# Regrouping the value and score products of layer 2 into four 32-wide groups, and moving its output product, in a four-layer cross-attention kernel

## The chip, the cores and the metric

The kernel runs on one core of a Trainium2 chip. The metric is the time of one execution on the device in microseconds (us), as the median of three runs. All arithmetic is in fp32. In this profile one fp32 matrix product appears as two MATMUL records and two weight loads; counts below are counts of records unless "product" is written.

## The reference

Input: `x` (4 sequences of 1024 rows, 256 wide), one context of 77 rows per sequence, and for layer 2 a weight and a mask for each score. Four layers follow one another; each has 16 heads.

- Layer 0: causal self-attention with the context appended, then a feed-forward block.
- Layer 1: a linear attention over the context beside a windowed self-attention (heads of 16).
- Layer 2, cut to what matters:

```python
q = (x @ Wq.T + bq)           # 16 heads of 16 columns
k = (ctx @ Wk.T + bk);  v = (ctx @ Wv.T + bv)      # 77 rows
scores = einsum('bhqd,bhkd->bhqk', q, k) / sqrt(16)
scores = where(mask, -inf, scores * attention_weights)
out = einsum('bhqk,bhkd->bhqd', softmax(scores), v)
x = layernorm(x + out @ Wo.T + bo) * gamma + beta
```

- Layer 3: rms norm, cross-attention with the same context with heads of 64, output product, and the sum with its input.

## The kernel before

The kernel first does layer 0 (to about 1090 us) and layer 1 (to about 1713 us), in steps of one sequence and four heads. Small jobs for later layers are spread over these steps by a planner: `jobs0(b, quad)` lists the jobs of layer 0's step for sequence `b` and heads group `quad`, each a generator with the number of its pieces and the part of the step in which they are due. Two of these jobs prepare layer 2 in DRAM, both in step (0, 0): `values2` multiplies the contexts with `Wv` and writes the values to `kept_v`, and `keys2` writes the keys to `kept_k`, four times, each time masked (`hsel4`) to every fourth head.

Layers 2 and 3 run together, in slots (`slot23`). Slot `i` works on row tile `i` of 128 rows in layer 2 (32 tiles) and on tile `j = i - 12` in layer 3. Each engine executes its instructions in the order in which the slot writes them; no scheduler changes it. A layer-2 tile passes through six slots:

- Slot `i`, `score2`: q times keys on TensorE into two PSUM tiles of two banks each (`pair_tile`, two buffers), multiplied with the weights by VectorE (L1545) into `s`, a buffer of 128 x 1232 (16 heads of 77), and masked (L1550). Then `maxima2` (L1554, L1558).
- Slot `i + 1`: `exps2` on ScalarE, 16 instructions (L1563); `sums_of` on VectorE (L1567, L1570); `divided` on GpSimd (L1574).
- Slot `i + 3`: `turned_into(p3, "pT2")`: ten transposes on TensorE (psT, L1375) in three groups, each evicted by ScalarE into `pT` (L1376).
- Slot `i + 4`: `values_of2`: values times `pT`, into `pvT`, copied to `oT` by ScalarE (L1593).
- Slot `i + 5`: `out2`: `oT` times `Wo` into `po2`; `add2` adds it to `x` on VectorE (L1602), then GpSimd adds `bo` (L1603).

Layer 3 in the same slots: `score3` (TensorE 16 records from G, then VectorE L1626 and L1627 for each of two halves), `exp3` on ScalarE (L1643), `sums_of` and `divided` one slot later, then `turned_into(c2, "pT3")` (the same lines L1375, L1376) and `out3` (20 records from U and pT, added to `x` at L1639) two slots later. `po2` and `po3` share one PSUM buffer. `psT`, `pvT` and other small PSUM tiles share a pool of three buffers (`sm`). From slot 9 on, `between` (called through `more()`, once in four slots for four tiles) does the layer norm of layer 2 and the rms norm of layer 3: bn_stats on VectorE, powers on GpSimd (L293), ScalarE (L1502), `xn` on VectorE (L316), transposes, and L1442. `prep2` computes q of the next sequence.

TensorE's order in a slot that has all of this is: transposes of layer 3, `score2`, `out3`, `values_of2`, `score3`, transposes of layer 2, `out2`.

The values lie for `values_of2` as 11 blocks of up to 128 rows of `s` by 128 columns: each row of `s` (one head and one context row) has its head's 16 columns filled and zeros elsewhere. `score2` makes four products per tile, each with 64 rows of q (four heads) against keys that are masked to one head in each of four blocks, 308 columns.

Of the kernel before, what the change touches and what calls it, by code (L numbers as in the profile page):

```python
# [17 lines left out]
P = 128  # L18
# [13 lines left out]
def tile_xattn_seq(ctx: ExitStack, tc: tile.TileContext, d: dict, out: bass.AP):  # L32
# [13 lines left out]
    def mm(o, lhsT, rhs, start=True, stop=True, **kw):  # L46
        n = 1
        for k in rhs.shape[1:]:
            n *= k
        put[0] += n / 600.0  # L50
        nc.tensor.matmul(o, lhsT, rhs, start=start, stop=stop, **kw)  # L51
# [475 lines left out]
    def pair_tile():  # L527
        return big.tile([P, 2, 512], F32, name="ps", tag="big")
# [403 lines left out]
    kept_g = dram.tile([P, 2, 8, 2, NS], F32, name="kept_g")  # L932
    kept_u = dram.tile([NB, H, S, D], F32, name="kept_u")

    HALF, DIAG = HH * S * P, S * P + DH
    kept_v = dram.tile([NB, 2, HH * DIAG], F32, name="kept_v")
    stg = wpool.tile([P, 1024], F32, name="stg", tag="s7")
    turn = [0]

# [25 lines left out]

    def values2():

        n = NB * 2 * HH * DIAG // P // 8
        nc.gpsimd.memset(stg[:, 0:n], 0.0)
        nc.sync.dma_start(  # L970
            out=kept_v.rearrange("b e x -> (b e x)").rearrange("(p k n) -> p k n", p=P, n=n),
            in_=stg[:, 0:n].unsqueeze(1).to_broadcast([P, 8, n]),
        )
        yield
        for b in range(NB):
            pk = sm.tile([S, D], F32, name="pk", tag="sm")
            for c in range(2):
                mm(pk, ctxT[:, b, c, :], l2["Wv"][:, c, :], start=(c == 0), stop=(c == 1))
            v = place(3, NS)[:S, 0:D]
            nc.vector.tensor_tensor(v, pk, rows["bv2"][:S], ALU.add)  # L980
            for e in range(2):
                to = kept_v[b, e].rearrange("(j x) -> j x", x=DIAG)[:, 0 : S * P]
                nc.sync.dma_start(
                    out=to.rearrange("j (s p) -> s j p", p=P)[:, :, 0:DH],
                    in_=v[:, P * e : P * e + P].rearrange("s (j r) -> s j r", r=DH),
                )
            yield

    def keys2():
# [376 lines left out]
    def rows_in(c):  # L1366
        return P if c < NC - 1 else HSIZE
# [10 lines left out]
    def new_scores(tag, bufs):  # L1378
        s = late.tile([P, P * NC], F32, name=tag, tag=tag, bufs=bufs)
        nc.gpsimd.memset(s[:, HK:], 0.0)  # L1380
        return s
# [27 lines left out]

    def loads2(b):  # L1410

        V = late.tile([P, NC + 1, P], F32, name="V2", tag="V2", bufs=2)
        lo, hi = [kept_v[b, e, 0:HALF].rearrange("(r n) -> r n", n=P) for e in range(2)]

        k = HH * S % P
        nc.gpsimd.memset(V[:, 4:6, :], 0.0)
        nc.sync.dma_start(
            out=V[:, 0:4, :], in_=lo[0 : 4 * P].rearrange("(c p) n -> p c n", p=P)
        )
        nc.sync.dma_start(out=V[0:k, 4, :], in_=lo[4 * P :])  # L1420
        nc.sync.dma_start(out=V[k:P, 5, :], in_=hi[0 : P - k])
        nc.sync.dma_start(
            out=V[:, 6:10, :], in_=hi[P - k : 5 * P - k].rearrange("(c p) n -> p c n", p=P)
        )
        nc.sync.dma_start(out=V[0:HSIZE, 10, :], in_=hi[5 * P - k :])
        shared["v2", b] = V
        yield

    def half_rows(e):
        return slice(64 * e, 64 * e + 64)  # L1430
# [95 lines left out]
    def score2(a, i):  # L1526

        b, t = a["b"], a["t"]
        qT, kb = shared["b2", b], shared["k2"]
        assert shared["ready2"] >= b  # L1530
        fs, mk = shared.pop(("side", i))
        if i + 1 < NB * NT:
            load_sides(i + 1)
        s = a["s"] = new_scores("s2", 4)
        for o in range(2):
            ps = pair_tile()
            for e in range(2):
                r = half_rows(e)
                mm(
                    ps[:, e, 0 : 4 * S].rearrange("p (h s) -> p h s", s=S),  # L1540
                    qT[r, o, P * t : P * t + P],
                    kb[r, o, :, b, :],
                )
            so = slice(o * HH * S, (o + 1) * HH * S)
            nc.vector.tensor_tensor(  # L1545
                s[:, so].rearrange("p (i n) -> p i n", i=2), ps[:, :, 0 : 4 * S],
                fs[:, so].rearrange("p (i n) -> p i n", i=2), ALU.mult,
            )
        sv = s[:, 0:HK]
        nc.vector.copy_predicated(sv, mk, low.to_broadcast([P, HK]))  # L1550
# [33 lines left out]
    def values_of2(a):  # L1584

        V = shared["v2", a["b"]]
        pv = sm.tile([P, 2, P], F32, name="pvT", tag="sm")
        for k in range(NC + 1):
            o, c = (0, k) if k < 5 else (1, k - 1)
            r = slice(0, rows_in(c))  # L1590
            mm(pv[:, o, :], V[r, k, :], a["pT"][r, c, :], start=k in (0, 5), stop=k in (4, NC))
        oT = a["oT"] = late.tile([P, 2, P], F32, name="oT", tag="oT", bufs=2)
        nc.scalar.copy(oT, pv)  # L1593

# [50 lines left out]
    def slot23(i, two, three, more):  # L1645

        n = NB * NT
        j = i - LAG
        if i < n:
            two[i] = dict(zip("bt", divmod(i, NT)))  # L1650
        if 0 <= j < n:
            three[j] = dict(zip("bt", divmod(j, NT)))
        a, p1, p3, p4, p5 = (two.get(i - k) for k in (0, 1, 3, 4, 5))
        c, c1, c2 = (three.get(j - k) for k in range(3))
        if j < 0:
            if p1:
                exps2(p1, range(H))
            score2(a, i)
            more()
            if p5:  # L1660
                out2(p5)
            if p4:
                values_of2(p4)
            maxima2(a)
            more()
            if p3:
                turned_into(p3, "pT2")
            if p5:
                add2(p5)
            more()  # L1670
            if p1:
                sums_of(p1, "den2")
                divided(p1)
            more()
        elif i < n + 5:
            if c2:
                turned_into(c2, "pT3")
            if p1:
                exps2(p1, range(4))
            if a:  # L1680
                score2(a, i)
            if c1:
                sums_of(c1, "den3")
                divided(c1)
            if p1:
                exps2(p1, range(4, 8))
            more()
            if c2:
                out3(c2)
            if p1:  # L1690
                exps2(p1, range(8, 12))
            if a:
                maxima2(a)
            if p4:
                values_of2(p4)
            more()
            if p1:
                exps2(p1, range(12, H))
            if c:
                score3(c, j)  # L1700
            more()
            if p3:
                turned_into(p3, "pT2")
            if c:
                exp3(c)
            if p1:
                sums_of(p1, "den2")
            if p5:
                out2(p5)
                add2(p5)  # L1710
            more()
            if p1:
                divided(p1)
        else:
            if c1:
                sums_of(c1, "den3")
                divided(c1)
            for o in range(2):
                if c2:
                    turned_into(c2, "pT3", (o,))  # L1720
                if c:
                    score3(c, j, (o,))
                if o == 0:
                    more()
            if c2:
                turned_into(c2, "pT3", (2,))
            more()
            if c:
                exp3(c)
            if c2:  # L1730
                out3(c2)
            more()
        two.pop(i - 5, None)
        three.pop(j - 2, None)
# [15 lines left out]
    def jobs0(b, quad):  # L1750
# [7 lines left out]
        if b == 0 and quad == 0:  # L1758
            j.append(Job(later_constants(), 3, 0.0, 0.4))
            j.append(Job(keep("c00", None), 1, 0.1, 0.2, us=0.85))  # L1760
            j.append(Job(values0(0, 0), 8, 0.2, 0.8, us=0.43))
            j.append(Job(other_contexts(), 3, 0.0, 0.1))
            j.append(Job(feature_weights(), 3, 0.5, 1.0))
            j.append(Job(values2(), 5, 0.3, 0.9, us=0.85))
            j.append(Job(keys2(), 4, 0.5, 0.9, us=0.5))
        if (b, quad) == (0, 1):
            j.append(Job(heads3("wk"), 8, 0.0, 1.0, us=1.03))
# [138 lines left out]
    def more():  # L1906
        for e in list(live2):
            gen, each = e[:2]
            for _ in range(each):
                got = next(gen, StopIteration)  # L1910
                if got is StopIteration:
                    live2.remove(e)
                if got:
                    break
# [49 lines left out]
```

## Time and profile before

| What | us |
|---|---|
| median of 3 runs | 2309.76 (2304.88 to 2311.91) |
| the profiled execution | 2310.56 |
| its span in the profile | 2308.8 |
| TensorE busy / VectorE busy / ScalarE busy / GpSimd busy | 2158.3 / 1506.8 / 1027.5 / 652.2 |
| mean granted TensorE clock | 0.982 of full speed |
| layer 2's value products (pvT), busy, 704 records | 90.9 (78.5 + 12.4) |
| layer 2's score products (ps from kb and qT), busy, 256 records | 42.9 |
| first score product of layer 2 / last pvT record | starts at 1724.3 / 2207.3 |

Engines: PE is TensorE's matmul, PEld its weight load, DVE VectorE, ACT ScalarE, POOL GpSimd, SP the engine that issues the DMAs. L51 is the helper through which almost all products go, so products are told apart by their tiles: `po<-U,pT` is `out3`, `po<-w2q,oT` is `out2`, `ps<-G,xT` is `score3`, `ps<-kb,qT` is `score2`. A form such as `128*32 128x192` means 128 rows contracted, 32 weight columns, 192 columns streamed. "Idle before" is the time that an engine stood still ahead of an instruction, and the name behind the arrow is what it waited for.

### The profile page before, as it was taken

What the parts mean: (1) busy time and instruction counts of PE and PEld (TensorE: products, weight loads), DVE (VectorE), ACT (ScalarE), POOL (GpSimd) and SP (SyncE); (2) the same over time, 40 slices, a digit from 0 to 9 for tenths busy, and PEclk for the clock granted to TensorE, in tenths of its full rate; (3) what the DMA queues carried; (4) which work ended last, traced back from release to release, by engine and by line L of the source; (5) the groups of instructions that cost most, each with busy time, mean ns of one, the idle gap of its engine ahead of it and who ended that gap; (6) DMA issues with size and microseconds to landing.
All of it is one profiled execution on the core that took longest, in us unless ns stands there. A gap on an engine that the chain in (4) does not pass through costs nothing.

```text
span 2308.8 us, 41140 instructions
## 1 busy us (share of the span) xinstructions
PE 2158.3 (93%) x16842; PEld 1358.9 (59%) x16874; DVE 1506.8 (65%) x2476; ACT 1027.5 (45%) x1716; POOL 652.2 (28%) x959
## 2 busy tenths in 40 slices
PE   4999999999999999999989999999988899999999
PEld 2544444555555455554556665666656678788877
DVE  3756567755566455754375666777748888788654
ACT  1144444434444444344533444544547655555322
POOL 2011113111131112310152233333333444444432
PEclk9899999999999999999989999999999999999999
DMA  7221121100000000101000010111025412313000
GB/s 217 55 57 68 31 65 41 40 6 15 7 15 2 10 11 6 38 1 19 6 15 6 15 26 16 21 20 20 15 74 152 136 51 68 100 49 95 10 10 17
DMA packets 87858, 93.98 MB, mean 41 GB/s; under 512 B 35714, under 2 KB 77558, under 8 KB 87542
## 3 DMA queue, kind: packets, MB, share of 16 engines
q1 hardware_dynamic: 87670, 91.35, 15.2%
q8 instruction: 133, 2.18, 0.4%
q14 instruction: 55, 0.45, 0.1%
HBM read 55.31 MB, written 18.39 MB: 32 GB/s over the span
## 4 chain that ended last, share of the span: by engine, by line
PE 67%; DVE 15%; ACT 4%; issue 2%; POOL 2%; DMA 0%; DVEq 0%; ACTq 0%; POOLq 0%; SPq 0%
PE ps L51 26%; PE po L51 12%; PE pv L51 6%; PE pp L51 5%; PE ph L51 4%; DVE mpart L672 3%; PE pvT L51 2%; DVE ms L1138 2%; PE ppv L51 2%; PE psT L1375 2%; PE pvw L51 1%; DVE mrow L1142 1%; PE pm L590 1%; PE pt L607 1%; ACT pe L738 1%
## 5 line engine op out<-in xcount | busy, mean ns | idle before, releaser
L51 PE MATMUL ps<-qk 32*128 32x192 f32 (+9 forms) x6528 | 581.8, 428 | 57.9 <-DVE mpart L672 25.1
L738 ACT ACTIVATE pe<-ps 128x1024 f32<-128x1024 f32 (+2 forms) x384 | 363.3, 952 | 589.5 <-PE ps L51 579.9
L51 PEld LDWEIGHTS ps<-qk 32*128 32x128 f32 (+1 forms) x6528 | 315.8, 185 | 295.6 <-issue 75.3
L672 DVE TENSOR_REDUCE mpart<-ps 128x2 f32<-128x1024 f32 (+4 forms) x384 | 331.0, 885 | 241.6 <-PE ps L51 240.8
L741 POOL TENSOR_SCALAR_AFFINE_SELECT pe<-pe 128x256 f32<-128x256 f32 (+1 forms) x192 | 95.2, 497 | 665.3 <-ACT pe L738 664.3
L1214 ACT ACTIVATE pew<-ps 128x768 f32<-128x768 f32 x128 | 103.4, 812 | 196.4 <-PE ps L51 196.4
L1574 POOL TENSOR_TENSOR s<-s,den 128x1232 f32<-128x1232 f32 x64 | 144.2, 2254 | 130.2 <-DVE den L1570 125.2
L1219 POOL TENSOR_SCALAR_AFFINE_SELECT pew<-pew 128x512 f32<-128x512 f32 x128 | 81.9, 640 | 337.7 <-ACT pew L1214 337.6
L1138 DVE TENSOR_TENSOR ms<-ps,maskw 128x768 f32<-128x768 f32 x128 | 122.1, 954 | 69.6 <-PE ps L51 68.1
L51 PE MATMUL po<-U,pT 128*128 128x256 f32 (+1 forms) x640 | 147.2, 385 | 10.8 <-DVE x L1602 7.6
L51 PE MATMUL pv<-pe,va 128*32 128x512 f32 (+3 forms) x1536 | 157.1, 496 | 0.0
L51 PE MATMUL ph<-yT,w 128*128 128x256 f32 x512 | 143.1, 401 | 2.4 <-DVE va L401 1.0
L51 PEld LDWEIGHTS po<-U,pT 128*128 128x128 f32 (+1 forms) x640 | 120.3, 192 | 35.0 <-ACT pT L1376 19.6
L51 PEld LDWEIGHTS po<-w,hT 128*128 128x128 f32 x800 | 111.8, 193 | 47.7 <-issue 38.9
L51 PE MATMUL ps<-G,xT 128*128 128x308 f32 x512 | 139.2, 422 | 0.0
L51 PE MATMUL po<-w,hT 128*128 128x128 f32 (+1 forms) x800 | 138.1, 317 | 0.9 <-ACT hT L904 0.9
L1563 ACT ACTIVATE s<-s,nm 128x77 f32<-128x77 f32 x512 | 134.8, 358 | 5.9 <-DVE nm L1558 5.9
L1376 ACT COPY pT<-psT 128x512 f32<-128x512 f32 (+1 forms) x192 | 87.7, 522 | 105.8 <-PE psT L1375 105.2
L665 DVE TENSOR_REDUCE mpart<-ps 128x8 f32<-128x1024 f32 x64 | 78.2, 1225 | 82.6 <-PE ps L51 80.0
L51 PEld LDWEIGHTS ph<-yT,w 128*128 128x128 f32 x512 | 88.8, 192 | 64.0 <-issue 50.8
L1142 DVE TENSOR_REDUCE mrow<-ms 128x4 f32<-128x768 f32 x128 | 122.2, 955 | 4.4
L51 PEld LDWEIGHTS ps<-G,xT 128*128 128x128 f32 x512 | 94.3, 190 | 30.1
(202 smaller groups left out, 3297.6 us busy)
## 6 DMA issues: line engine op xcount, KB each, us to landing
side<-in_fside_t SPq DMA_DIRECT2D x32, 616.0 KB
qk<-st SPq DMA_DIRECT2D x256, 64.0 KB
side<-in_mask_t SPq DMA_DIRECT2D x32, 154.0 KB
G<-kept_g SPq DMA_DIRECT2D x4, 1232.0 KB
U<-kept_u SPq DMA_DIRECT2D x4, 1152.0 KB
x<-in_x SPq DMA_DIRECT2D x8, 512.0 KB
out<-x SPq DMA_DIRECT2D x32, 128.0 KB
kept_g<-st SPq DMA_DIRECT2D x22, 154.0 KB
```

The source lines that it names most:

```text
L51: nc.tensor.matmul(o, lhsT, rhs, start=start, stop=stop, **kw)
L665: nc.vector.tensor_reduce(mpart[self.own][:, :, 2 * p : 2 * p + 2, 0].rearrange("p t j -> p j t"), ps.rearrange("p j (t n) -> p j t n", n= ...
L672: nc.vector.tensor_reduce(mpart[bl][:, i, 2 * p : 2 * p + 2, ci], ps[:, :, o : o + w], axis=AX.X, op=ALU.max,)
L738: nc.scalar.activation(pp[:n, :, o:512], ps[:n, :, o:512], AF.Exp, scale=SC)
L741: nc.gpsimd.affine_select(out=own, in_=own, compare_op=ALU.is_ge, fill=0.0, base=0, pattern=[[0, 2], [0, k], [1, P]], channel_multiplier=-1,)
L1138: nc.vector.tensor_tensor(v, ps.rearrange("p j (i n) -> p j i n", i=2)[:, :, :, 0:n], (maskw[:, 1:2] if w else maskw).unsqueeze(1).to_broa ...
L1142: nc.vector.tensor_reduce(mo, v, axis=AX.X, op=ALU.max, negate=True)
L1214: nc.scalar.activation(pp[:, :, :, 0 : P + WIN], ps.rearrange("p j (i n) -> p j i n", i=2)[:, :, :, 0 : P + WIN], AF.Exp, scale=SC,)
L1219: nc.gpsimd.affine_select(out=pf[:, :, 0:P], in_=pf[:, :, 0:P], compare_op=ALU.is_ge, fill=0.0, base=0, pattern=[[0, 4], [1, P]], channel_ ...
L1376: nc.scalar.copy(pT[:, 4 * group : 4 * group + n, :], ps[:, 0:n, :])
L1563: nc.scalar.activation(hs, hs, AF.Exp, bias=a["nm"][:, h : h + 1], scale=SC)
L1574: nc.gpsimd.tensor_tensor(s3, s3, a["den"].unsqueeze(2).to_broadcast([P, H, S]), ALU.mult)
```

## The change

Four parts:

1. The values are laid out in groups of two heads, 32 columns. `CUTS` lists the 17 meetings of a group's 154 rows of `s` with a block of 128 rows of `s`. `values2` writes a compact `kept_w` (one row for each row of `s`, 32 columns); a new job, `spread2`, copies it in 17 DMAs from DRAM to DRAM into `kept_v`, one block of 128 x 32 for each cut, with zeros around. `values_of2` makes 17 products of 128 rows by 32 columns against 128 columns of `pT`. Four groups follow one another in turn and write to the four quarters of `pvT`'s partitions. `loads2` loads V by one DMA where five DMAs and a memset did it.
2. `score2` makes eight products with 32 rows of q (two heads), 154 columns each, four row groups in turn, into the four banks of both pair tiles; VectorE's two multiplications come after all eight and take two row groups each.
3. In the slots with both layers, `out2` and `add2` stand in front of layer 2's transposes; before, they stood after the transposes, `exp3` and `sums_of`.
4. `spread2` and `keys2` are jobs of step (0, 1); `keys2` was in step (0, 0).

```diff
+    PAIR = 2 * S
+    CUTS = [
+        (c, q, max(P * c, PAIR * q), min(P * c + P, PAIR * q + PAIR))
+        for q in range(HH) for c in range(PAIR * q // P, (PAIR * q + PAIR - 1) // P + 1)
+    ]
+    kept_w = dram.tile([NB, HK, HP], F32, name="kept_w")
+    kept_v = dram.tile([NB, P, len(CUTS), HP], F32, name="kept_v")
...
+    def spread2():
+        for k, (c, q, lo, hi) in enumerate(CUTS):
+            nc.sync.dma_start(
+                out=kept_v[:, lo - P * c : hi - P * c, k, :], in_=kept_w[:, lo:hi, :]
+            )
+            yield
...
     def loads2(b):
-        V = late.tile([P, NC + 1, P], F32, name="V2", tag="V2", bufs=2)
...
+        V = late.tile([P, len(CUTS), HP], F32, name="V2", tag="V2", bufs=2)
+        nc.sync.dma_start(out=V, in_=kept_v[b])
...
+        pair = [pair_tile() for _ in range(2)]
         for o in range(2):
-            ps = pair_tile()
-            for e in range(2):
-                r = half_rows(e)
+            for g in range(4):
+                e = 2 * (g % 2)
                 mm(
-                    ps[:, e, 0 : 4 * S].rearrange("p (h s) -> p h s", s=S),
-                    qT[r, o, P * t : P * t + P],
-                    kb[r, o, :, b, :],
+                    pair[g // 2][:, g % 2, PAIR * o : PAIR * o + PAIR].rearrange(
+                        "p (h s) -> p h s", s=S
+                    ),
+                    qT[rows_of(g), o, P * t : P * t + P], kb[rows_of(g), o, e : e + 2, b, :],
+                    skip_group_check=True,
                 )
...
-        for k in range(NC + 1):
-            o, c = (0, k) if k < 5 else (1, k - 1)
-            r = slice(0, rows_in(c))
-            mm(pv[:, o, :], V[r, k, :], a["pT"][r, c, :], start=k in (0, 5), stop=k in (4, NC))
+        for o in range(2):
+            own = [
+                [(k, c) for k, (c, q, _, _) in enumerate(CUTS) if q == 4 * o + j] for j in range(4)
+            ]
+            for n in range(max(map(len, own))):
+                for j in range(4):
+                    if n < len(own[j]):
+                        k, c = own[j][n]
+                        mm(
+                            pv[rows_of(j), o, :], V[:, k, :], a["pT"][:, c, :],
+                            start=(n == 0), stop=(n == len(own[j]) - 1), skip_group_check=True,
+                        )
...
             if c:
                 score3(c, j)
             more()
+            if p5:
+                out2(p5)
+                add2(p5)
             if p3:
                 turned_into(p3, "pT2")
             if c:
                 exp3(c)
             if p1:
                 sums_of(p1, "den2")
-            if p5:
-                out2(p5)
-                add2(p5)
             more()
...
+        if (b, quad) == (0, 1):
+            j.append(Job(spread2(), len(CUTS), 0.1, 0.9))
             j.append(Job(keys2(), 4, 0.5, 0.9, us=0.5))
```

More of the change, by code (lines that the diff above doesn't have):

```diff
@@ L933, in tile_xattn_seq @@
     kept_u = dram.tile([NB, H, S, D], F32, name="kept_u")
-    HALF, DIAG = HH * S * P, S * P + DH
-    kept_v = dram.tile([NB, 2, HH * DIAG], F32, name="kept_v")
+    PAIR = 2 * S
[5 more added lines that the diff above has]
+    kept_v = dram.tile([NB, P, len(CUTS), HP], F32, name="kept_v")
     stg = wpool.tile([P, 1024], F32, name="stg", tag="s7")
@@ L966, in values2 @@
     def values2():
-        n = NB * 2 * HH * DIAG // P // 8
+        n = len(CUTS) * HP
         nc.gpsimd.memset(stg[:, 0:n], 0.0)
         nc.sync.dma_start(
-            out=kept_v.rearrange("b e x -> (b e x)").rearrange("(p k n) -> p k n", p=P, n=n),
-            in_=stg[:, 0:n].unsqueeze(1).to_broadcast([P, 8, n]),
+            out=kept_v.rearrange("b p k n -> p b (k n)"),
+            in_=stg[:, 0:n].unsqueeze(1).to_broadcast([P, NB, n]),
+        )
+        nc.sync.dma_start(
+            out=kept_w.rearrange("b (s q) n -> s b (q n)", s=S),
+            in_=stg[:S, 0 : H * HP].unsqueeze(1).to_broadcast([S, NB, H * HP]),
         )
@@ L981, in values2 @@
             for e in range(2):
-                to = kept_v[b, e].rearrange("(j x) -> j x", x=DIAG)[:, 0 : S * P]
                 nc.sync.dma_start(
-                    out=to.rearrange("j (s p) -> s j p", p=P)[:, :, 0:DH],
-                    in_=v[:, P * e : P * e + P].rearrange("s (j r) -> s j r", r=DH),
-                )
+                    out=kept_w[b].rearrange("(q e s) n -> e s q n", e=2, s=S)[e, :, :, DH * e : DH * e + DH],
+                    in_=v.rearrange("s (q e r) -> s q e r", e=2, r=DH)[:, :, e, :],
+                )
+            yield
+    def spread2():
+        for k, (c, q, lo, hi) in enumerate(CUTS):
+            nc.sync.dma_start(
+                out=kept_v[:, lo - P * c : hi - P * c, k, :], in_=kept_w[:, lo:hi, :]
+            )
             yield
@@ L1410, in loads2 @@
     def loads2(b):
-        V = late.tile([P, NC + 1, P], F32, name="V2", tag="V2", bufs=2)
[L1413 to L1425, printed above, removed]
+        V = late.tile([P, len(CUTS), HP], F32, name="V2", tag="V2", bufs=2)
+        nc.sync.dma_start(out=V, in_=kept_v[b])
         shared["v2", b] = V
@@ L1534, in score2, with of_pair @@
         s = a["s"] = new_scores("s2", 4)
+        pair = [pair_tile() for _ in range(2)]
         for o in range(2):
-            ps = pair_tile()
-            for e in range(2):
-                r = half_rows(e)
-                mm(
-                    ps[:, e, 0 : 4 * S].rearrange("p (h s) -> p h s", s=S),
-                    qT[r, o, P * t : P * t + P],
-                    kb[r, o, :, b, :],
-                )
-            so = slice(o * HH * S, (o + 1) * HH * S)
+            for g in range(4):
+                e = 2 * (g % 2)
+                mm(
+                    pair[g // 2][:, g % 2, PAIR * o : PAIR * o + PAIR].rearrange(
[3 more added lines that the diff above has]
+                    skip_group_check=True,
+                )
+        def of_pair(v, k):
+            v = v[:, 0:HK].rearrange("p (o g n) -> p g o n", o=2, g=4)
+            return v[:, 2 * k : 2 * k + 2]
+        for k in range(2):
             nc.vector.tensor_tensor(
-                s[:, so].rearrange("p (i n) -> p i n", i=2), ps[:, :, 0 : 4 * S],
-                fs[:, so].rearrange("p (i n) -> p i n", i=2), ALU.mult,
+                of_pair(s, k),
+                pair[k][:, :, 0 : 2 * PAIR].rearrange("p i (o n) -> p i o n", o=2),
+                of_pair(fs, k), ALU.mult,
             )
@@ L1587, in values_of2 @@
         pv = sm.tile([P, 2, P], F32, name="pvT", tag="sm")
-        for k in range(NC + 1):
-            o, c = (0, k) if k < 5 else (1, k - 1)
-            r = slice(0, rows_in(c))
-            mm(pv[:, o, :], V[r, k, :], a["pT"][r, c, :], start=k in (0, 5), stop=k in (4, NC))
+        for o in range(2):
[9 more added lines that the diff above has]
+                            start=(n == 0), stop=(n == len(own[j]) - 1), skip_group_check=True,
+                        )
         oT = a["oT"] = late.tile([P, 2, P], F32, name="oT", tag="oT", bufs=2)
```

## The prediction

> **What bounds the kernel now.** I read the page first: TensorE is busy 93% of the span, so a cut in its work can count, but the share is a mean over the layers. The change works on layers 2 and 3, 1713 to 2309 us, so I then took the busy time by stretches. The columns after the stretch's length are busy us (and records) of PE, PEld, DVE, ACT and POOL, then clock and DMA.
>
> ```profile
> PE 2158.3 (93%) x16842; PEld 1358.9 (59%) x16874; DVE 1506.8 (65%) x2476; ACT 1027.5 (45%) x1716; POOL 652.2 (28%) x959
> ```
>
> ```profile
> 1724.00:1854.59 130.59, 113.38 (x650) 84.63 (x649) 109.93 (x150) 89.17 (x282) 49.07 (x60) 0.92 0.45 134
> 2024.51:2088.67 64.16, 62.66 (x368) 52.29 (x369) 56.80 (x83) 34.34 (x101) 30.54 (x37) 1.00 0.18 58
> 2152.84:2215.26 62.42, 58.58 (x326) 49.70 (x327) 32.71 (x57) 20.97 (x50) 26.22 (x31) 0.97 0.03 9
> ```
>
> Before slot 13 VectorE is nearly as busy as TensorE. The second row is one cycle of four full slots: TensorE 62.66 of 64.16, VectorE 56.80. So VectorE caps the gain of such a cycle at 7.4 us. Third, the chain of waits, for that cycle:
>
> ```profile
> 2051.08 1.09 PE psT L1375 x10
> 2052.17 0.86 PE po L51 x4
> 2053.03 0.89 PE psT L1375 x8
> 2053.98 1.08 ACT x L1502 x2
> 2055.59 4.59 PE po L51 x20
> 2060.17 2.46 PE pvT L51 x22
> 2062.63 4.16 PE ps L51 x16
> 2070.49 1.05 POOL rs L293
> 2072.30 2.86 DVE xn L316 x3
> ...
> 2086.62 1.35 DVE den L1567
> 2088.67 4.56 PE po L51 x20
> ```
>
> I measure a slot from one `out3` start to the next: 2024.51, 2039.96, 2055.59, 2071.56, 2088.67, so 15.45, 15.63, 15.97 and 17.11. The first is all TensorE: 4.52 `out3` + 2.46 pvT + 4.15 `score3` + 1.09 psT + 0.87 `out2` + 1.09 psT + 1.24 `score2` = 15.42. The fourth is VectorE's, from xn to den. Last, the timeline of the seam between two slots:
>
> ```profile
> 2051.61 1.35 ACT L1376 COPY pT<-psT 128x512 f32<-128x512 f32 x3 [3.27 <-PE psT L1375]
> 2052.84 1.24 ACT L1643 ACTIVATE s<-s 128x1232 f32<-128x1232 f32 x1
> 2053.98 1.08 ACT L1502 ACTIVATE x<-x,away,rs 128x256 f32<-128x256 f32 x2
> 2054.97 1.33 ACT L1376 COPY pT<-psT 128x512 f32<-128x512 f32 x3
> ```
>
> ScalarE does, in this order, pT2's copies, `exp3`, sometimes two L1502, and pT3's copies, which `out3` needs. This string is what TensorE meets next when it gets faster.
>
> **Values (saves 1.40 per tile).** The 22 records cost 2.46. After, there are 34, of the form 128*32. Layer 1 has that form, with four partition groups in turn, and the other form too, 32*128:
>
> ```profile
> 1500.46 0.75 PE L51 MATMUL pvw<-pew,va 128*32 128x192 f32 x16
> 1501.14 0.66 PE L590 MATMUL pm<-ident,mrow 128*128 128x128 f32 x4
> 1502.61 0.94 PE L51 MATMUL ps<-qk 32*128 32x192 f32 x16
> 1503.48 0.38 PE L51 MATMUL ppv<-w1v,xT 128*128 128x128 f32 x1
> ```
>
> From start to next start, 16 records of 192 columns take 0.68, 42.5 ns each; one 128*128 record of 128 columns takes 2.46 / 22 = 112 ns. So the four groups overlap. By columns, 128 / 192 x 42.5 = 28.3 ns, x34 = 0.96, and 0.1 for the one group with three cuts, which is alone at its end: 1.06. If records don't shrink with columns: 42.5 x 34 = 1.45. Saving 1.40, bounds 1.0 and 1.5; I take the first because full records scale with columns: 308 of them (ps from G) take 139.2 / 512 = 272 ns, 2.4 times the 112 of 128.
>
> One rule speaks against this. The Trainium skill, "TensorEngine Tiling (Array Packing)", Key Properties, says that a change of tiling mode drains TensorE; the change adds two mode changes per tile around pvT. In the rows above the mode changes between the pvw records and the 128*128 record behind them, which starts 0.68 after the first of 16: a drain there is inside the 42.5 ns that I price by. If each change cost one full record's 0.27 us more, 64 of them would add 17 us.
>
> **Scores (saves 0.44).** 8 records in 1.24 become 16 of the form 32*128 with 154 columns. 16 with 192 took 0.87 (1502.61 to 1503.48); by columns 0.70. I take 0.80. VectorE keeps two multiplications of 616 elements (784 ns each); the first now waits for six of eight products, 0.6 us instead of half of 1.24, so no later. Both pair tiles were used by this step before.
>
> **`out2` in front (a loss on ScalarE's string, a gain on VectorE's).** Its 0.87 on TensorE is the same. Let T be the end of `score3`. Before: psT2 T to 1.09, `out2` to 1.96, psT3 to 3.05, `score2` to 4.29, then `out3`. After: `out2` to 0.87, psT2 to 1.96; pT2's copies start 0.69 after psT2 (2050.91 to 2051.61 in the timeline) at 1.56 and end at 2.91; `exp3` to 4.15; the first pT3 copy 0.6 later and 0.1 to start: `out3` at 4.85, although TensorE is ready at about 4.2. So a plain slot changes by 0.55 - 1.40 = -0.85; `score2`'s saving is hidden. In the slot with L1502 (1.08 more on ScalarE) `out3` goes from T + 4.5 to T + 5.85: -0.05. In the third slot `out3` waited 0.49 for L1602, since `po2` and `po3` share a buffer and `add2` stood behind the sums; that wait is gone (`add2` is earlier): 4.78 to 4.85, so -1.33. In the fourth VectorE does 17.1 of work either way, and `out3` follows through L1627, `exp3`, pT3's copy: 0. A cycle: -2.2.
>
> **The sum**, against the execution's own 2310.56:
> - three such cycles (1887.61, 2024.51, 2088.67): -6.6.
> - the cycle with `prep2` from 1952.23: two slots of 19.9 and 19.3 where 1.72 us products of q give ScalarE time: -1.84 each (1.40 + 0.44); then -1.3 and 0: -5.0.
> - 1854.59 to 1887.61, two slots: -1.3.
> - slots 12 and 13: `prep2` again, -1.6 each: -3.2.
> - slots 32 to 35 (no `score2`): -1.40 each, but `out3` goes from T + 3.7 to 4.1 to T + 4.75: -2.
> - slots 0 to 11: the chain holds one pvT and three score pieces, 1.40 + 3 x 0.44 = 2.7; VectorE (109.9 of 130.6) takes up part: -1.5.
> - Layer 0: `keys2` moves. Its 8 VectorE instructions of 587 ns (4.7 us) leave 70 to 95 us, where VectorE is busy over 9 of 10, and its TensorE work (3.4 us there, where the clock is 0.72 to 0.77) goes to a step where TensorE is busy 9.7 of 10. Bounds -4.7 and +3.4; I take 0, since both steps trade one engine for the other.
> - `spread2`: 17 issues on SP between the qk writes, of about 0.4 us. Some 4900 runs of 128 bytes; 1232 runs of 64 bytes of kept_v kept the DMA engines for about 1.5 us, so 6 to 12 us spread over a step of 55. The last qk write starts at 148 and its step begins after 156, so 0; 3 if that cover fails.
> - V's loads: five DMAs and a memset become one, four times, one slot ahead or more: 0. `load_sides` stays ahead of it in SP's queue.
>
> Sum -19.6: 2291.0. The median shown is 0.8 under this execution: **2290**.
>
> **Rivals.**
> 1. *ScalarE's string doesn't hold* (0.14). If `exp3` finds ScalarE free, TensorE's 1.84 comes off until VectorE's floor: about -6 in 4.5 cycles, -3.5 and -5.6 around them: -36, 2274. For it: VectorE is at 89% and can fill more. Against: the order of ScalarE's program.
> 2. *Little is left* (0.16): pvT at 1.45 and L1502 in the seam of two slots per cycle: a cycle gives about 0, and the `prep2` and border slots keep -6: 2304.
> 3. *Slower, by `out2`'s place* (0.14). Every slot's `out3` waits behind pT2's copies and `exp3`. It costs 0.55 in a plain slot and 1.35 with L1502; if every one of 24 slots paid 1.35 (+32) while pvT gave 1.0 in 15 of them (-15), the result is +17: 2327. It decides from the point where the added wait for pT exceeds pvT's saving. For it: ScalarE's chain is already met in the slot at 2055.59. Against: only one slot in four has L1502 there.
> 4. *The groups don't overlap* (0.02): 34 x 112 ns = 3.8, +1.35 a tile, 2340. The pvw row speaks against it.
>
> **How the numbers follow.** My forecast has 0.54. Its own range is 2282 to 2299 (pvT 1.0 to 1.5, layer 0 by -4.7 to +3.4). A measurement of this kernel can tell about 0.3%, 6.9 us, from no change, so faster means under 2302.8. Faster: forecast and rival 1, and a quarter of rival 2: 0.72. Same: the rest of rival 2 and a little of rival 3: 0.14. Slower: 0.14. The range 2272 to 2315 leaves out most of rivals 3 and 4 and the tail of rival 1.
>
> **What would show it.** pvT's 34 records within 1.0 to 1.5 us a tile; `score2` 0.7 to 0.9; the idle time of `out3` behind DVE L1602 (6.3 us from 1900 to 2220) gone, and behind ACT pT (3.1) grown to 10 or more; full cycles of about 62. I am wrong if cycles come near 58 (rival 1), if pvT takes over 2 us, if `out3` waits over 1 us for pT in most slots, or if layers 0 and 1 end more than 5 us away from before.

## The result and the profile after

The changed kernel takes 2323.68 us (median of 5 runs, 2316.99 to 2325.98) against 2309.85 for the kernel before: a ratio of 1.0056, 95% interval 1.0035 to 1.0076. By that ratio it is slower by 12.9 us (13.8 between the medians), where 2290 was forecast. The profiled execution has a span of 2321.7 (before 2308.8). Two executions of the record, one of e9's kernel (2664.38 us, mean clock 0.748) and one of the kernel before (2490.98 us, 0.842), fell in a slower state and are left out of the ratios.

TensorE's busy time fell by 21.6 us all the same. The page's first part:

```profile
PE 2136.7 (92%) x17514; PEld 1315.1 (57%) x17514; DVE 1505.9 (65%) x2476; ACT 1026.8 (44%) x1716; POOL 650.0 (28%) x955
```

So the work was removed, and time was added elsewhere. Cut by place, with the boundaries read from the timeline (slots run from one `out3` start to the next; the differences are taken before rounding):

| Place | before | after | difference | forecast |
|---|---|---|---|---|
| start to layer 2's first score product | 1724.3 | 1746.3 | +22.1 | 0 |
| from there to the first `out3` | 130.3 | 130.6 | +0.4 | -4.7 |
| the next 18 slots | 298.3 | 292.9 | -5.4 | -12.9 |
| slots 32 to 35 | 62.4 | 58.5 | -4.0 | -2 |
| the rest | 93.5 | 93.4 | -0.2 | 0 |

**Layer 0.** The waits of SP's queue, before and after, and then of TensorE after, between 60 and 190 us (total, times, longest):

```profile
SPq L80 <- PE pk L51: 7.5, 1, 7.5
```

```profile
SPq L80 <- PE pk L51: 61.1, 1, 61.1
```

```profile
PE ps L51 <- DMA qk<-st: 17.7, 1, 17.7
```

L80 is the load of layer 3's `Wo`. After the change it stood for 61.1 us at the head of SP's queue, until the last product of `keys2` (`pk`). The buffer of that load (tag `s3`) is the one that holds layer 2's `Wk`, which `keys2` reads. What followed is in SP's timeline, after first and before second:

```profile
85.14 0.81 SPq L991 DMA_DIRECT2D kept_w<-st  x2
147.13 0.40 SPq L80 DMA_DIRECT2D l3wo<-in_L_wo  x1
147.77 0.68 SPq L1000 DMA_DIRECT2D kept_v<-kept_w  x1
148.50 3.96 SPq L792 DMA_DIRECT2D qk<-zrow  x1
152.52 2.48 SPq L377 DMA_DIRECT2D qk<-kc  x4
155.03 2.11 SPq L1000 DMA_DIRECT2D kept_v<-kept_w  x3
157.25 2.52 SPq L377 DMA_DIRECT2D qk<-st  x4
159.81 5.79 SPq L1000 DMA_DIRECT2D kept_v<-kept_w  x7
...
166.61 3.12 SPq L1000 DMA_DIRECT2D kept_v<-kept_w  x4
169.84 2.46 SPq L377 DMA_DIRECT2D qk<-st  x4
```

```profile
94.79 0.40 SPq L80 DMA_DIRECT2D l3wo<-in_L_wo  x1
...
112.92 35.23 SPq L377 DMA_DIRECT2D qk<-st  x8
```

After, nothing leaves SP from 86 to 147 us. Then the next step's q and k (`qk<-st`), which were spread over 112.92 to 148.15 before, go out among fifteen copies of `spread2`, whose issues alone take 0.68 + 2.11 + 5.79 + 3.12 = 11.7 us. The last four q writes are out at 172.3, and TensorE starts at 172.78.

The wait has a second price. TensorE's clock falls during it and is still at 0.50 when the work goes on. Busy time by stretches, after first, then e1, whose edit is told below and whose TensorE doesn't wait there (columns as in the prediction: PE, PEld, DVE, ACT, POOL, clock, DMA):

```profile
172.78:178.50 5.72, 5.72 (x24) 2.03 (x28) 1.12 (x1) 1.02 (x1) 0.00 (x0) 0.50 0.78 202
```

```profile
157.70:164.50 6.80, 6.33 (x62) 3.01 (x54) 4.26 (x6) 4.15 (x6) 0.28 (x1) 1.00 0.67 169
```

At half clock 5.72 us do the work of 2.86, so about 2.9 us are lost on top of the 17.7.

**The slots.** A full cycle of four (stretch, busy us and records of PE, PEld, DVE, ACT, POOL, clock, DMA), and the stretch that answers to the first one of before:

```profile
1746.30:1876.90 130.60, 100.73 (x889) 70.16 (x888) 110.53 (x150) 87.92 (x282) 48.24 (x58) 0.88 0.44 129
2042.33:2106.01 63.68, 59.52 (x449) 47.20 (x449) 55.96 (x83) 34.34 (x101) 30.65 (x36) 0.97 0.19 59
```

TensorE lost 3.1 us of busy time in a cycle, and the cycle only 0.5. The chain of waits for it names the string through ScalarE that was forecast: transposes, pT's copies, `exp3` ("issue"), pT's copy, `out3`:

```profile
2042.33 6.18 PE po L51 x20
...
2054.06 0.86 PE po L51 x4
2054.93 0.45 PE psT L1391 x4
2055.45 0.62 ACT pT L1392 x2
...
2056.41 0.39 ACT pT L1392
2056.86 0.95 issue
2057.81 0.61 ACT pT L1392
2058.46 4.59 PE po L51 x20
```

The waits of `out3` from layer 2's start to slot 36 confirm it: on pT they grew from 3.1 to 17.1. On L1602 (now L1622) they fell from 10.7 to 6.3; three waits, of up to 3.5 us, are left. Before first, then after:

```profile
PE po L51 <- DVE x L1602: 10.7, 12, 2.7
...
PE po L51 <- ACT pT L1376: 3.1, 6, 1.6
```

```profile
PE po L51 <- ACT pT L1392: 17.1, 21, 3.2
...
PE po L51 <- DVE x L1622: 6.3, 3, 3.5
```

What was not forecast is the chain's first row: this `out3` takes 6.18, the next one 4.59. The same 20 records are slower because of the clock. Busy time by stretches of 2 us (the clock is the third number from the end):

```profile
2040.00:2042.00 2.00, 0.79 (x12) 0.56 (x12) 2.00 (x3) 1.43 (x2) 0.73 (x1) 1.00 0.00 0
2042.00:2044.00 2.00, 1.67 (x4) 1.40 (x5) 1.86 (x4) 2.00 (x8) 1.42 (x1) 0.54 0.00 0
2044.00:2046.00 2.00, 2.00 (x7) 1.59 (x7) 1.97 (x2) 2.00 (x9) 0.91 (x2) 0.60 0.00 0
2046.00:2048.00 2.00, 2.00 (x11) 1.77 (x10) 1.18 (x2) 0.03 (x1) 0.64 (x1) 1.00 0.00 0
```

TensorE's timeline just ahead of it:

```profile
2036.44 2.71 PE L1391 MATMUL psT<-ident,s 128*128 128x128 f32 x20
2039.08 0.53 PE L51 MATMUL ps<-kb,qT 32*128 32x154 f32 x4
2040.53 0.79 PE L51 MATMUL ps<-kb,qT 32*128 32x154 f32 x12 [0.92 <-DVE s L1647]
2042.33 6.18 PE L51 MATMUL po<-U,pT 128*128 128x256 f32 x20 [1.00 <-ACT pT L1392]
```

At the end of VectorE's slot TensorE has little left to do: it waits 0.92 in the score products (they need both pair tiles, and `score3` still holds one) and 1.00 before `out3`. Then the clock is at half, and that costs 1.6. Cut more finely, the granted clock is 0.50 from 2042.17 to 2045.58, 3.4 us, and 1.00 on either side. It happens in three of the five cycles after, and once before, from 1850 us to the end (at 2152.84, an `out3` of 6.24).

### The profile page after: what moved, and what is told of

Its sections match the earlier page's. It is cut to its first block, busy times and chain, and to the rows that moved or that the text cites. A ratio compares the mean times of both kernels' runs of the same rounds, so it can differ in the third digit from the quotient of the medians.

```text
span 2321.7 us, 42492 instructions
## 1 busy us (share of the span) xinstructions
PE 2136.7 (92%) x17514; PEld 1315.1 (57%) x17514; DVE 1505.9 (65%) x2476; ACT 1026.8 (44%) x1716; POOL 650.0 (28%) x955
## 4 chain that ended last, share of the span: by engine, by line
PE 65%; DVE 15%; ACT 6%; issue 2%; POOL 2%; DVEq 0%; ACTq 0%; POOLq 0%
PE ps L51 25%; PE po L51 12%; PE pv L51 6%; PE pp L51 6%; PE ph L51 4%; DVE mpart L672 3%; DVE ms L1154 2%; PE ppv L51 2%; PE pvw L51 1%; DVE mrow L1158 1%; PE pm L590 1%; PE pt L607 1%; ACT pe L738 1%; PE pvT L51 1%; ACT pT L1392 1%
## 5 line engine op out<-in xcount | busy, mean ns | idle before, releaser
L51 PE MATMUL ps<-qk 32*128 32x192 f32 (+9 forms) x6528 | 589.9, 431 | 73.1 <-DVE mpart L672 23.2
L51 PEld LDWEIGHTS ps<-qk 32*128 32x128 f32 (+1 forms) x6528 | 319.1, 186 | 313.3 <-issue 93.2
L51 PE MATMUL po<-U,pT 128*128 128x256 f32 (+1 forms) x640 | 150.8, 392 | 17.2 <-ACT pT L1392 17.1
L51 PE MATMUL pv<-pe,va 128*32 128x512 f32 (+3 forms) x1536 | 158.0, 498 | 0.0
L51 PE MATMUL ph<-yT,w 128*128 128x256 f32 x512 | 145.8, 407 | 2.4 <-DVE va L401 1.0
L51 PEld LDWEIGHTS po<-U,pT 128*128 128x128 f32 (+1 forms) x640 | 122.6, 196 | 38.9 <-ACT pT L1392 22.6
L51 PE MATMUL ps<-G,xT 128*128 128x308 f32 x512 | 140.7, 426 | 0.0
L51 PE MATMUL po<-w,hT 128*128 128x128 f32 (+1 forms) x800 | 137.6, 316 | 0.9 <-ACT hT L904 0.9
L51 PEld LDWEIGHTS po<-w,hT 128*128 128x128 f32 x800 | 111.4, 192 | 47.7 <-issue 38.9
L51 PEld LDWEIGHTS ph<-yT,w 128*128 128x128 f32 x512 | 90.3, 195 | 65.1 <-issue 51.6
L51 PEld LDWEIGHTS ps<-G,xT 128*128 128x128 f32 x512 | 94.2, 190 | 33.1 <-issue 2.4
```

## The experiments

Four edits were taken apart: the place of `keys2`, the values (with `spread2`), the scores, and `out2` in front. Each ratio is to runs of the kernel before that were made beside it. "Slots" is the time of the 18 slots in the table above, and "half clock" the number of `out3` between 1850 and 2170 us that took over 6 us.

| Kernel | median us | ratio to before [95%] | first score product | slots | half clock |
|---|---|---|---|---|---|
| before | 2309.85 | 1 | 1724.3 | 298.3 | 1 |
| after (all four) | 2323.68 | 1.0056 [1.0035, 1.0076] | 1746.3 | 292.9 | 3 |
| e1: without `keys2`'s move | 2302.39 | 0.9969 [0.9955, 0.9983] | 1728.2 | 293.1 | 3 |
| e2: all four, `l3wo` loaded later | 2302.44 | 0.9969 [0.9954, 0.9984] | 1726.2 | 293.0 | 3 |
| e3: all four, `spread2` later | 2309.36 | 0.9999 [0.9985, 1.0013] | 1732.7 | 293.2 | 3 |
| e4: `keys2`'s move alone | 2316.03 | 1.0024 [1.0009, 1.0039] | 1729.5 | 298.6 | 1 |
| e5: values and scores | 2295.07 | 0.9946 [0.9928, 0.9964] | 1723.2 | 286.4 | 1 |
| e6: e1 with filler products | 2303.03 | 0.9973 [0.9962, 0.9985] | 1721.9 | 290.2 | 0 |
| e7: values and `out2` | 2297.72 | 0.9951 [0.9933, 0.9969] | 1721.8 | 288.1 | 0 |
| e8: `out2` alone | 2315.93 | 1.0032 [1.0019, 1.0046] | 1720.2 | 302.2 | 0 |
| e9, e11: values alone | 2291.75 | 0.9918 [0.9903, 0.9933] | 1722.6 | 284.9 | 0 |
| e10: scores alone | 2312.13 | 1.0005 [0.9994, 1.0015] | 1728.3 | 299.5 | 2 |

The first score product starts anywhere from 1720.2 to 1728.3 in before, e8 and e10, whose layers 0 and 1 are the same. So a single profile says nothing of some 4 us up or down there. The slots repeat better: after, e1, e2 and e3 have the same code in them and take 292.9 to 293.2, before and e4 298.3 and 298.6.

**e1, e2: free SP's queue in two ways.** e1 puts `keys2` back:

```diff
+            j.append(Job(keys2(), 4, 0.5, 0.9, us=0.5))
         if (b, quad) == (0, 1):
             j.append(Job(spread2(), len(CUTS), 0.1, 0.9))
-            j.append(Job(keys2(), 4, 0.5, 0.9, us=0.5))
```

> The changed kernel with keys2 back in step (0, 0); spread2 stays in step (0, 1). Theory W: the load of l3wo takes the buffer of layer 2's Wk, so with keys2 moved it waits on SP for keys2's last product at 147 us, and all that SP has behind it (qk's clears and writes, spread2) stands for 61 us. Then the load is issued at about 90 to 95 us, TensorE's wait of 17.7 us for qk's write is gone, and the time is about 2303 us (2323.7 less 17.7 and a few us behind it). Theory S: the 17 DMAs of spread2 on SP hold up qk's writes by themselves. Then the wait stays over 10 us and the time within 2316 to 2326.

e2 leaves `keys2` where the change put it, and loads `l3wo` a step later:

```diff
-            if (b, quad) == (0, 1):
-                load3("wo", wpool, "s3")
             if (b, quad) == (0, 2):
                 load3("wv", wpool, "s4")
+                load3("wo", wpool, "s3")
```

> The changed kernel with the load of l3wo issued in step (0, 2), behind l3wv, in place of step (0, 1); keys2 and spread2 stay in step (0, 1). Theory W: nothing on SP waits for keys2's products ahead of qk's writes, the wait of 17.7 us is gone, about 2303 us. Theory S: no difference, 2316 to 2326 us.

Both give 2302.4. In e1's waits the wait for the buffer is back near its old size, and TensorE waits for no qk write:

```profile
SPq L80 <- PE pk L51: 6.0, 1, 6.0
```

e2 shows that the keys' work in step (0, 1) costs nothing of its own: only the load that stands behind it does. All 17 copies of `spread2` are still in step (0, 1) in both kernels, so they aren't the cause by themselves.

**e3, e4: the standing queue without the copies.** e3 moves `spread2` to step (0, 2); e4 is the kernel before with `keys2` in step (0, 1).

```diff
-        if (b, quad) == (0, 1):
+        if (b, quad) == (0, 2):
             j.append(Job(spread2(), len(CUTS), 0.1, 0.9))
+        if (b, quad) == (0, 1):
             j.append(Job(keys2(), 4, 0.5, 0.9, us=0.5))
```

> The changed kernel with spread2 in step (0, 2); keys2 stays in step (0, 1), so SP still stands until 147 us. Theory W, with spread2 as the second half of the delay: after 147 us SP needs about 13 us for l3wo, the clears, kc and the eight qk writes (0.6, 4.0, 2.5, 2.5, 0.9, 2.5), so TensorE waits about 6 us in place of 17.7 and the time is about 2312 us. Theory S: no wait, about 2303 us.

```diff
+        if (b, quad) == (0, 1):
             j.append(Job(keys2(), 4, 0.5, 0.9, us=0.5))
```

> The kernel before with keys2 alone moved to step (0, 1). Theory W: SP stands until about 147 us for keys2's last product, TensorE then waits about 6 us for qk's write: about 2316 us. Theory S: no spread2, no wait, 2310 us within noise.

SP stands for 61.1 us in both. In e3, TensorE then waits 2.5 us for the qk write:

```profile
PE ps L51 <- DMA qk<-st: 2.5, 1, 2.5
```

In e4 it stands still for 2.7 at the same product, which the profile puts down to "issue". About 6 us were expected in both, so that the times come near those of theory W (2312 and 2316) isn't due to the wait alone. The rest is again the clock. In e3:

```profile
157.70:164.50 6.80, 6.80 (x30) 2.20 (x30) 2.72 (x3) 2.86 (x4) 0.00 (x0) 0.50 0.90 282
```

These 6.8 us at half clock lose 3.4; e4 has the same from 158.1 to 164.9, and e1 1.00 in that place (above). Wait and clock make 5.9 and 6.1 us. By the ratios e3 is 6.9 us above e1 and e4 5.5 above before (2 to 9). The 17.7 us of the changed kernel need both parts: the queue that stands, and the copies that come out of it in a bunch ahead of the last qk writes.

**e5, e8: `out2` in front, undone and alone.** e5 is e1 with:

```diff
             more()
-            if p5:
-                out2(p5)
-                add2(p5)
             if p3:
                 turned_into(p3, "pT2")
...
                 sums_of(p1, "den2")
+            if p5:
+                out2(p5)
+                add2(p5)
             more()
```

> The kernel of e1 with out2 and add2 back behind the sums. Theory string (the forecast's walk): pT2's copies start 0.87 us earlier, exp3 and pT3's copies with them, out3 starts 4.0 us after score3's end in place of 4.85, a plain slot goes from 14.54 to about 13.95 us, the slot with L1502 from 15.5 to 14.7, VectorE's slot stays: about -10 us, 2292. Theory L1602: with a faster TensorE out3 waits for add2, which stands behind the sums again; the waits of 10.7 us in the kernel before come back or grow, and the time is 2302 to 2308 us.

The slots take 286.4 instead of 293.1. Both theories hold in part, and the 2295 lies between theirs. By the string's walk the plain slot falls from 14.54 to 13.84 and the one with L1502 from 15.51 to 14.89, but the slot that waits for L1602 grows from 14.54 to 14.92. The waits of `out3` change sides, and their sum stays as large. The clock falls once instead of three times, which is about 3.2 of the 6.7 us:

```profile
PE po L51 <- DVE x L1622: 18.3, 13, 3.5
```

e8 makes the opposite edit in the kernel before:

> The kernel before with out2 and add2 in front of the turned weights, nothing else. Theory string: a plain slot +0.55 us, the slot with L1502 +1.35, the slot that waited for L1602 +0.1, VectorE's 0, the four slots of tiles 32 to 35 about +0.8: some +11 us, 2322. Theory L1602: the 10.7 us of waits for add2 go: 2300.

The slots grow by 3.9 us: the plain one from 15.38 to 15.76, the one with L1502 from 15.7 to 16.56, while the one that waited for L1602 falls from 15.97 to 15.76. `out2` in front is a loss in both settings; with nothing else changed the ratio is 1.0032. That is about 7 us by the ratio, where theory string had 11.

**e6: keep TensorE busy.** e1 with three overwritten products ahead of `out3`, in the places where TensorE waits behind VectorE's slot:

```diff
         po = pvp.tile([P, D], F32, name="po3", tag="pv")
+        if a["t"] % 4 == 2:
+            for k in range(3):
+                mm(po, ident, U[:, k, :])
```

> The kernel of e1 with three products of 256 columns, whose result is overwritten, ahead of out3 in one slot of four, the slot behind VectorE's. Theory clock: out3 takes 6.2 us there in place of 4.6 because TensorE stood idle and its clock went to about half; the fillers (1.3 us) fill the idle time, out3 takes 4.6 to 4.8 us, and three such slots give back 1.6 us each less some 0.3 of filler that is in the way: -4 us, 2298. Theory pT: out3's 6.2 us are waits between its records for pT's copies. Then the fillers only add to it: 0 to +4 us.

In its timeline the filler lies where the wait was, and `out3` behind it takes 4.48:

```profile
1882.88 0.79 PE L51 MATMUL ps<-kb,qT 32*128 32x154 f32 x12 [0.87 <-DVE s L1647]
1883.60 1.56 PE L51 MATMUL po<-U,ident 128*128 128x256 f32 x6
1885.00 4.48 PE L51 MATMUL po<-U,pT 128*128 128x256 f32 x20
```

No `out3` falls to half clock. The three slots behind a dip give back 5.1 us, but the slots ahead of the fillers' `out3` take 2.3 more, so the 18 slots take 2.9 us less than in e1. From the nineteenth `out3` on the fillers stand in TensorE's path and cost 2.3, so the median doesn't move (-4 was expected). The filler shows what the low clock costs; as a remedy it would have to be kept to the slots with both layers.

**e7, e10: the scores, undone and alone.** e7 is e1 with the four score products of before; e10 is before with the eight new ones.

> The kernel of e1 with score2 as in the kernel before (four products with 64 rows). Theory string: score2's saving of 0.43 us a tile is hidden in plain slots behind pT3's copies and counts in the four slots with prep2 alone: 2303 to 2305 us. Rival, TensorE's sum counts: 32 x 0.43 = 14 us, 2316. Rival, the new form does harm (both pair tiles are claimed at once, TensorE waited 4.4 us for them): 2298 to 2301.

> Only the new score products are put into the kernel before: old values, out2 behind, keys2 in step (0,0). Theory: they take 0.4 off TensorE per tile, hidden where out3 waits for pT or L1602, and shown in plain slots: slots 15.4 and 15.7 fall by 0.2 to 0.4, 2303 to 2308. Rival: the wait for both pair tiles and for all eight products costs by itself, slots of VectorE grow from 17.1 to 17.5 and out3 behind them runs at half clock (6.2 instead of 4.6) once in a cycle: 2313 to 2316.

With the old scores no `out3` runs at half clock, and the slots fall from 293.1 to 288.1, as the rival had it in which the new form does harm: the three slots behind a dip give back 4.1 us and VectorE's five slots 2.2, while the others take 1.3 more. In e10 the new scores take 0.8 us instead of 1.24, the plain slot falls from 15.38 to 14.89, but VectorE's slot grows from 17.12 to 17.37 or more and the clock falls twice; `out3` waits more for VectorE:

```profile
PE po L51 <- DVE x L1611: 17.7, 13, 3.4
```

The slots take 1.1 us more than before, and the time is that of before. The new scores bring nothing alone, and cost 4 to 5 us where values and `out2` are changed too.

**e9, e11: the values alone.** The kernel before with the new values, and `spread2` in step (0, 1); nothing else:

```diff
+        if (b, quad) == (0, 1):
+            j.append(Job(spread2(), len(CUTS), 0.1, 0.9))
```

> Only the new values and spread2 (in step (0,1)) are put into the kernel before: the old scores, out2 behind the sums, keys2 in step (0,0). If the three findings so far add up (keys2 back, out2 back about 7, old scores about 5), the time is 2288 to 2292, the slots from the first out3 to the nineteenth take 283 to 286 and no out3 in them takes 6.2. Rival: the new scores do harm only where out2 stands in front, since there both push the idle time to one place; then out2 back has already mended all, and it is as with the new scores and out2 back, 2295 and 286. Clean saving of the value products: 1.25 a tile in the plain slots, so 15.4 to 15.7 becomes 14.2 to 14.5, VectorE's slot stays at 17.1.

It has the lowest median of all, in the range that was expected if the three findings add up. e11 is the same kernel once more, for its profile:

> The kernel with the new values alone once more, for a profile at full clock: plain slots 14.2 to 14.9, VectorE's slot 17.1 to 17.4, 283 to 287 from the first out3 to the nineteenth; no wait of SP's queue at l3wo's load above 7; no out3 of 6.2 in the plain cycles if the idle time of TensorE behind VectorE's slot is as in the kernel before.

The cycle is 14.92, 17.20, 14.33, 14.65, where before has 15.97, 17.12, 15.38, 15.70 (the timeline's starts; the prediction's 15.45 and 15.63 come from the chain): a fall of 1.05 in each slot but VectorE's, where 1.25 was expected. The timelines show where 0.2 went. Before first, then e11; from start to start, the rows are `out3`, pvT, `score3`, and what follows:

```profile
2039.89 4.59 PE L51 MATMUL po<-U,pT 128*128 128x256 f32 x20
2044.31 2.62 PE L51 MATMUL pvT<-pT,V 128*128 128x128 f32 x22
2046.77 4.31 PE L51 MATMUL ps<-G,xT 128*128 128x308 f32 x16
2050.91 1.25 PE L1375 MATMUL psT<-ident,s 128*128 128x128 f32 x10
```

```profile
1911.96 4.59 PE L51 MATMUL po<-U,pT 128*128 128x256 f32 x20 [0.22 <-ACT pT L1392]
1916.47 1.28 PE L51 MATMUL pvT<-pT,V 128*32 128x128 f32 x34
1917.68 4.41 PE L51 MATMUL ps<-G,xT 128*128 128x308 f32 x16
1921.93 1.25 PE L1391 MATMUL psT<-ident,s 128*128 128x128 f32 x10
```

pvT falls from 2.46 to 1.21. But `out3` ahead of it goes from 4.42 to 4.51, and `score3` behind it from 4.14 to 4.25: 0.20 in all. In e11's single records the added time lies at the two changes of form: from `out3`'s last record to pvT's first 0.307 instead of 0.215, and from `score3`'s first to its second 0.363 instead of 0.264; all later steps of `score3` are 0.259 as before. The second change also shows ahead of `score3`, inside pvT's 1.21: from pvT's last record to `score3`'s first 0.202 instead of 0.110. The rule on mode changes in the Trainium skill, "TensorEngine Tiling (Array Packing)", Key Properties, agrees with these rows as far as they go: time is added at each change, 0.09 us at the first and 0.19 at the second. That it is a drain, no row shows.

## Why the prediction was wrong

**The step that failed: `keys2`, "I take 0".** The step weighed VectorE's and TensorE's load in the two steps (bounds -4.7 and +3.4), and that part was right: in e2 the move costs nothing. It left out the buffer. `load3("wo", wpool, "s3")` is issued at the start of step (0, 1) and takes the buffer of `Wk`; while `keys2` was in step (0, 0), that wait lasted 7.5 us, and the profile of before had it as a row (SPq L80 <- PE pk L51). Moved a step later, the last reader of `Wk` held that load, and with it everything behind it on SP's queue, for 61.1 us. The ratio goes from 0.9969 (e1) to 1.0056: 20 us, which TensorE's wait of 17.7 and the half clock behind it, about 2.9, account for. The prediction's own sign for this, layers 0 and 1 more than 5 us away from before, came: they end 22 us later.

**The step beside it: `spread2`, "0; 3 if that cover fails".** The cover was read from before, where the last qk write is issued by 148.15. It failed together with the queue, and the issues, 0.8 us each where 0.4 was used, then came in front of the qk writes: 17.7 us of waiting instead of 3. In e1 and e11, where the queue doesn't stand, TensorE waits for no qk write in spite of `spread2`.

**`out2` in front: right slots, in part by luck.** Forecast were a plain slot of 14.6, one with L1502 of 15.6, one without the wait for L1602 of 14.64, VectorE's at 17.1. After shows 14.54 where the clock holds, 15.51, 14.54 and 17.5. But e8's added waits, 0.38 and 0.86, are under the 0.55 and 1.35 that were used, and the values' 1.05 is under 1.40. In the plain slot the two errors cancel, together with 0.18 of the scores' saving that was to be hidden.

**The missing terms in the slots: the clock, and VectorE's slot.** 16.1 to 16.2 instead of 14.54 in one slot of three cycles, about 5 us of the 7.5 that are missing between first `out3` and slot 32. VectorE's slot, put at 0, grew by 0.4 to 0.6 five times, 2.3 us; that comes with the new scores (without `prep2`, it is at least 17.37 in e10, and 17.12 to 17.21 in e7, e8 and e11). The other differences nearly cancel. The clock was not in the sum, though the profile of before had one such `out3`. e6 and e7 show it from two sides.

**Values: mechanism right, a quarter of the term didn't come.** Forecast 1.40 a tile, measured 1.25 in pvT and 1.05 in the slot. The row from layer 1 was misread: of its 16 records only eight have 192 columns, as the view of that tile from 1500.4 to 1501.2 shows.

```profile
L51 PE MATMUL pvw<-pew,va x16: 272/300/350, 1500.5 to 1500.9; 128*32 128x192 f32 x8, 128*32 128x128 f32 x8
```

So 42.5 ns is the price of 160 columns on the mean. By columns that is 34 ns for 128, 1.16 for 34 and 1.26 with the 0.1 for the group that ends alone: a saving of 1.20, near the 1.25. The 34 records come at 30.5 ns from start to start. The 0.20 between pvT and the slot is the changes of form in the neighbours, which had been priced inside the 42.5 ns; in layer 1 too a part of it lies behind the 0.68 (pm's second record starts 0.164 after its first, the later ones 0.109). The lower bound of 1.0 held. **Scores:** 0.81 was forecast at 0.80. That the saving is hidden holds for the slot with L1502 (15.51 in e7 and in after); in the two other slots 0.18 of it shows (14.72 in e7, 14.54). That VectorE's first multiplication starts "no later" was wrong: in its slot the products wait 0.92 for the second pair tile. **Slots 0 to 13** (-4.7 forecast): TensorE's busy time there fell from 113.38 to 100.73 with VectorE at 110 before and after, and the time didn't follow. The stretch takes 130.3 before, 130.4 to 130.7 in all six kernels with new values and new scores, and 128.2 to 129.1 where only one of the two, or neither but `out2`, is changed (e7, e8, e10, e11). What bounds that stretch was not settled. **Slots 32 to 35** gave -4.0 for -2.

**The rivals.** The time lies between the forecast and the third rival (2327), but not mainly for that rival's reason: `out2`'s place costs some 4 to 7 us, the queue 20. That the sum of -19.6 is nearly what the values bring alone (-18.9, from the ratio 0.9918) is chance: the sum counted them at 1.40 a tile and took a loss by `out2` off again. None of the three other edits gained anything, and together they cost 32 us (2323.68 against 2291.75).

## What to carry to other kernels

When a job is moved, list the buffers that it reads and who writes them next: a load that reuses such a buffer waits for the moved reader, and everything issued behind that load on its queue waits too. Count a cut on TensorE only up to the engine that ends the slot, and look at where the new idle time will lie, since gathered in one place it can cost clock in the work that follows. Of a change with several parts, time each part alone: here one part held all of the gain. And before a merged row of a profile is made a price, look up whether all its records have the same shape.

## What the runs showed that was not expected

- TensorE's clock fell to 0.50 for 3.4 us after only 1.9 us of idle time within 2.7 (the gaps around 0.92 and 1.00), and 20 records took 6.18 instead of 4.59. The size of the gap alone doesn't decide: in e5 gaps of 0.22 and 1.21 stand ahead of `out3` at 1885.96 (6.24) and at 2018.00 (4.56), and in after one gap of 3.19 ahead of the `out3` at 2169.85, which runs in 4.59. The three dips of after start at 1909.06, 2042.17 and 2107.03, and these are 39 and 19 times 3.413 us apart. So the clock may go by fixed stretches of that length, and what counts may be how much idle time falls in one of them; no run here settles it. The Trainium skill, "TensorE: Matmul & The Clock Gate", HAM oscillation, gives as its rule no idle gaps above about 3.4 us; these runs show the half clock behind gaps that are far shorter, which is nearer to what its next section tells of frequent short idle times.
- A change from 128*128 to 128*32 adds 0.09 us, the change back 0.19. Of these 0.28 us, 0.19 show in the records of the neighbouring products, so they are missed where only the changed product is timed.
- Fifteen DRAM-to-DRAM copies cost SP 11.7 us of issuing between 147.8 and 169.7 us, 0.8 each; the estimate had been 0.4.
- A wait of TensorE can cost more than its length: behind 17.7 us of standing still the clock stayed at 0.50 for 5.7 us of work, and behind 2.5 us in e3 it was 0.50 for 6.8 us.
